# A written order for layer 0's first blocks, 17 pieces in layer 1, and idle products at the layers' borders

## The chip, the core and the metric

The kernel runs on one core of one Trainium2 chip. A core has five engines that work side by side, each through its own queue of instructions in order: TensorE (PE in the profile) multiplies matrices, VectorE (DVE) and ScalarE (ACT) work element by element, GpSimd (POOL) does the same more slowly, and SyncE (SP) starts transfers. A product needs its weights loaded first; such a load is an instruction of its own (PEld) and overlaps the products. Data lies in an on-chip memory of 128 partitions, products are written to a small accumulator memory (PSUM), and transfers to and from the large memory (DRAM) run on 16 DMA engines that all queues share. ScalarE, GpSimd and SyncE can each start transfers.

The metric is device time in microseconds (us) of one execution. Times are medians of several runs; the profile is one execution more.

## The reference, cut to what matters

The input x is 8 samples of 128 channels and 56 x 56 pixels, all float32. Four layers follow one another, each x = x + layer(groupnorm(x)):

```python
# layer 0: attention between windows of 8 x 8 pixels (49 windows a sample)
proj = xw @ W_qkv + b_qkv                                  # q, k, v of each pixel
logit = einsum('npc,nqc->npq', q_win * SCALE, k_win)       # window means
topk_logit, r_idx = top_k(logit, 4)                        # 4 windows for each window
attn = softmax(einsum('bmqc,bmkc->bmqk', q_h * SCALE, k_sel))   # 8 heads, 64 x 256
out = (attn @ v_sel + depthwise3x3(v) + lepe_b) @ W_o + b_o
# layer 1: batch norm, then a recurrence over the 3136 pixels of a sample
inp = tanhshrink(seq @ w_in.T + b_in);  xgate = inp @ w_ih.T + b_ih + b_hh
h = tanh(xg + h @ w_hh.T)                                  # 512 states, pixel after pixel
out = h @ w_out.T + b_out
# layer 2: masked 3 x 3 and 1 x 1 convolutions;  layer 3: a residual block of two 3 x 3 convolutions
```

The group norm takes groups of 4 channels: mean and variance of each sample and group.

## The kernel before

All of x stays on the chip in one tile, X, of 128 channels by 8 samples by 3136 pixels.

**The beginning of layer 0** (lines 65 to 152 and 549 to 569). SyncE's queue loads the eight samples of x, 1.6 MB each, sample by sample. ScalarE's queue loads the constants and weights. Sample 0 is then prepared in program order; which instruction each engine takes next is left to the scheduler of the framework. `measure` (line 186) gives statistics of seven strips of 448 pixels (`bn_stats`, line 194), the mean over a group by a product with the constant matrix gavg (line 200), the variance likewise (line 213), and one over the root by an integer estimate and three rounds of four GpSimd steps (lines 218 to 229). `preparation` (line 233) has, for each strip: `normal` writes the normalised strip in window order (xw, line 244) and its window sums (xm, line 249); `keys` multiplies and VectorE adds the bias (line 258); `image` gives v as an image, evicted by ScalarE and stored by GpSimd's queue (lines 271 and 277); `pixels` gives v by pixel rows, evicted by VectorE and stored by GpSimd's queue (lines 293 and 297). Then `means` and `route` give the window logits, the four best windows and their numbers as one row, selr (line 329). Three strips of queries (line 345) follow. All this goes through four PSUM banks in turn (`psum`, line 180).

**The loop of layer 0** (lines 672 to 730). It works on pairs of windows, 196 in all, with an order written out by hand for PE, ScalarE, VectorE and GpSimd. SyncE's queue is left to the scheduler. Turn p of the loop computes scores, maxima and exponentials of pair p + 1 (lines 461, 469, 474), transposes them (line 497), and multiplies values of pair p (line 516). `gather` copies the chosen keys with GpSimd (line 436) and loads the chosen value rows by SyncE's queue (line 438, 8 transfers a pair). `divisors` spreads reciprocal sums by GpSimd (rc, line 485), which PE then transposes (line 506). Around this, the work of preparing later samples, the depthwise products (line 375) and output projections (line 401) is placed by a planner: `job(ready, due, ...)` enters a piece of work with the first turn in which it can run and the last in which it must, and each turn has places for one product evicted by VectorE, one more, and a light one. `hook(p, f)` calls f in turn p. These pieces share one PSUM bank, "pp". The loop begins at FIRST = -2, two turns ahead of the first values.

**Layer 1** (lines 736 to 949). The recurrence is cut into NCH = 19 pieces of TC = 166 pixels, which run side by side: with 8 samples, a step has 19 x 8 = 152 columns. Each piece starts WARM = 56 pixels ahead, so there are 56 warming steps and 166 true ones, 222 in all. Inputs of a pixel (xn, pi, inp) are computed for two steps at a time (`prepare`, line 814). In the 56 warming steps the gate inputs are stored (gk, line 870), since the last 56 pixels of a piece are those that the next piece warmed up on, and they are read back for the last 56 steps (`recall`, line 841). A step with new inputs has 8 input products and 16 hidden-state products (line 858); a repeated one has 16 and adds the stored inputs with VectorE (v, line 884). Outputs (po, line 893) are two steps wide. Each float32 product is two records in the profile. Before the recurrence stands a chain of small steps for the two norms (lines 753 to 780).

**Layer 2** begins with the statistics of sample 0 (line 1010), the norm, and copies that spread each padded image over four row groups (`spread`, line 1046), by ScalarE, SyncE's queue and GpSimd's queue.

Of the kernel before, what the change touches and what calls it, by code (L numbers as in the profile page):

```python
# [18 lines left out]
P = 128  # L19
B = 8  # L20
# [14 lines left out]
NCH = 19  # L35
TC = 166
# [8 lines left out]
def conv_stack_kernel(ctx: ExitStack, tc: tile.TileContext, a: dict, out: bass.AP):  # L45
# [19 lines left out]
    for b in range(2):  # L65
        nc.sync.dma_start(X[:, b, :], a["x"][b])
    gavg = load_const("gavg", [P, P])
    for b in range(2, B):
        nc.sync.dma_start(X[:, b, :], a["x"][b])
    mv1 = const.tile([P, B, 2], F32, name="mv1")  # L70
    root = const.tile([P, 1], F32, name="root")
# [50 lines left out]
    with ExitStack() as l0:  # L122
# [8 lines left out]
        ident = load_const("ident", [P, P], c0)  # L131
        hmask = load_const("hmask", [P, 2], c0)
        own = load_const("own", [P, P], c0)
        wqkv = c0.tile([P, 3 * P], F32, name="wqkv")
        nc.scalar.dma_start(wqkv, a["L0_conv_W_qkv"])
        wo = c0.tile([P, P], F32, name="wo")
        nc.scalar.dma_start(wo, a["L0_conv_W_o"])
        bqkv = c0.tile([P, 3], F32, name="bqkv")
        nc.scalar.dma_start(bqkv, a["L0_conv_b_qkv"].rearrange("(c p) -> p c", p=P))
        bv_row = c0.tile([P, P], F32, name="bv_row")  # L140
        nc.scalar.dma_start(
            bv_row, a["L0_conv_b_qkv"][2 * P : 3 * P].rearrange("(o c) -> o c", o=1).broadcast_to((P, P))
        )

        wlep = c0.tile([3 * CL, 3, 4, CL], F32, name="wlep")
        nc.scalar.dma_start(wlep, a["lepe_d"])
        lb = c0.tile([P, 1], F32, name="lb")
        nc.scalar.dma_start(lb, a["L0_conv_lepe_b"].rearrange("(p o) -> p o", o=1))
        bo = c0.tile([P, 1], F32, name="bo")
        nc.scalar.dma_start(bo, a["L0_conv_b_o"].rearrange("(p o) -> p o", o=1))  # L150
        bqs = c0.tile([P, 1], F32, name="bqs")
        nc.vector.tensor_scalar(bqs, bqkv[:, 0:1], QSCALE, None, ALU.mult)
# [25 lines left out]
        bank = itertools.count()  # L178

        def psum(b, shape, name):  # L180

            if b == 0:
                return ps_s.tile(shape, F32, name=name, tag=f"s{next(bank) % 4}")
            return ps_p.tile(shape, F32, name=name, tag="pp")

        def measure(b):
# [11 lines left out]
            def mean_mm():  # L198
                st["pm"] = psum(b, [P, 1], f"pm0_{b}")
                nc.tensor.matmul(st["pm"], gavg, mv[:, 0:1], start=True, stop=True)  # L200
# [10 lines left out]
            def var_mm():  # L211
                st["pv"] = psum(b, [P, 1], f"pv0_{b}")
                nc.tensor.matmul(st["pv"], gavg, st["e"], start=True, stop=True)

# [16 lines left out]
            return stats, fill(mean_mm, mean_end), fill(var_mm, var_end)  # L231

        def preparation(b):
# [3 lines left out]
            xm = samp.tile([P, NWIN], F32, name=f"xm_{b}", tag="xm", bufs=1)  # L237
            kT = samp.tile([P, NWIN, WPX], F32, name=f"kT_{b}", tag="kT")
            ks[b] = kT

            def normal(i):

                wins = slice(i * NW, (i + 1) * NW)
                nc.vector.tensor_scalar(
                    xw[:, wins, :].rearrange("p j (u v) -> p j u v", v=WS),
                    X[:, b, i * BLK : (i + 1) * BLK].rearrange("p (u j v) -> p j u v", u=WS, v=WS),
                    st["gm"], st["r"], ALU.subtract, ALU.mult,
                )
                nc.vector.tensor_reduce(xm[:, wins], xw[:, wins, :], AX.X, ALU.add)

            def keys_mm(i):
                st["pk", i] = psum(b, [P, BLK], f"pk_{b}_{i}")
                nc.tensor.matmul(  # L253
                    st["pk", i], wqkv[:, P : 2 * P], xwf[:, i * BLK : (i + 1) * BLK], start=True, stop=True
                )

            def keys_end(i):
                nc.vector.tensor_scalar(
                    kT[:, i * NW : (i + 1) * NW, :].rearrange("p w x -> p (w x)"), st["pk", i],
                    bqkv[:, 1:2], None, ALU.add,  # L260
                )

            def image_mm(i):
                st["pv", i] = psum(b, [P, BLK], f"pvt_{b}_{i}")
# [4 lines left out]
            def image_end(i):  # L269
# [6 lines left out]
                later.append(  # L276
                    lambda: nc.gpsimd.dma_start(vimg[b % 2][:, 1 + i * WS : 1 + (i + 1) * WS, :], t)
                )

            def pixels_mm(n):  # L280

                st["vp", n] = psum(b, [P, 4, P], f"pvp_{b}_{n}")
# [6 lines left out]
            def pixels_end(n):  # L289
                w0, pv = 8 * n, st["vp", n]  # L290
                t = strip.tile([P, 4, P], F32, name=f"vp_{b}_{n}", tag="vp")
                if n < NW - 1:
# [4 lines left out]
                    later.append(lambda: nc.gpsimd.dma_start(dst, t))  # L297
                else:
                    nc.vector.tensor_tensor(t[:WPX, 0, :], pv[:WPX, 0, :], bv_row[:WPX, :], ALU.add)
                    later.append(lambda: nc.gpsimd.dma_start(vpix[b % 2][w0], t[:WPX, 0, :]))  # L300


            def means_mm():
                st["pw"] = psum(b, [P, 2, NWIN], f"pw_{b}")
# [10 lines left out]
            def route_mm():  # L315
                st["pl"] = psum(b, [NWIN, NWIN], f"pl_{b}")
                nc.tensor.matmul(st["pl"], st["qk"][0], st["qk"][1], start=True, stop=True)

            def route_end():
# [17 lines left out]
                fill(route_mm, route_end),  # L337
            )

        def queries(b, i):  # L340
            st = {}

            def mm():
                st["pq"] = psum(b + i, [P, BLK], f"pq_{b}_{i}")
# [76 lines left out]

        def gather(W):
# [4 lines left out]
            _, idx = nc.values_load_multi_w_load_instructions(  # L427
                selrs[b][0:1, w * TOPK : (w + 1) * TOPK],
# [1088 lines left out]
```

## Time and profile before

| what | us |
|---|---|
| median of 3 runs | 3679.45 (3677.51 to 3683.7) |
| the profiled execution | 3677.05 |
| its span, first to last instruction | 3675.1 |
| first scores of layer 0 start at | 64.10 |
| last products of layer 0's loop | 1395.45 to 1396.47 |
| first input product of layer 1 | 1406.40 |
| last output product of layer 1 ends | 2935.9 |
| first product of layer 2's convolution | 2950.86 |
| layer 3, to the end | from about 3154 |

The profile names an instruction by its line in the kernel, its engine, its operation, and the tiles out<-in. Times are counted from the span's start. In a row of the timeline the bracket at the end is the time for which the engine had been idle before it, and what released it. The granted clock of PE is 1.00 at full speed and 0.50 at half.

### The profile page before, as it was taken

To read this page: it belongs to the slowest core of one execution; us is meant where nothing else is said; L and a number is where in the kernel's file an instruction comes from. 1 tells how busy PE (TensorE), PEld (TensorE's weight loads), DVE (VectorE), ACT (ScalarE), POOL (GpSimd) and SP (SyncE) were. 2 spreads that over 40 slices of the span, in tenths; PEclk is the share of its full clock that TensorE was granted. 3 is DMA by queue.
4 is the path that set the end of the run, shared out by engine and by line. 5 is a ranking of instruction groups with operands and counts; after the bars stand their busy time and mean duration, and the time that the engine had idled before them with its cause. 6 is when DMAs were issued, how large, how long until landed. Compare 5 with 4: busy or idle time off the path is not lost.

```text
span 3675.1 us, 85966 instructions
## 1 busy us (share of the span) xinstructions
PE 3545.7 (96%) x30150; PEld 2914.9 (79%) x30150; DVE 1889.8 (51%) x3923; ACT 1654.2 (45%) x5149; POOL 1349.3 (37%) x3663
## 2 busy tenths in 40 slices
PE   5999999999999998999999999999999989999998
PEld 3666666666666667999999999999999833799998
DVE  5888888888878773222111111111122266757665
ACT  2787878888888883222222222222211154122222
POOL 3767667676766662111111111111000066323221
PEclk8999999999999999999999999999999999999999
DMA  5444444343434431111000000000022166100000
GB/s 208 108 107 108 110 104 107 100 117 101 118 102 114 122 93 57 49 45 49 21 1 1 1 1 1 1 1 1 18 59 59 45 168 169 34 23 23 31 21 34
DMA packets 195814, 241.74 MB, mean 66 GB/s; under 512 B 42480, under 2 KB 153520, under 8 KB 194352
## 3 DMA queue, kind: packets, MB, share of 16 engines
q1 hardware_dynamic: 160992, 125.99, 11.8%
q0 software_dynamic: 32576, 109.48, 11.3%
q8 instruction: 245, 4.01, 0.5%
q14 instruction: 193, 1.58, 0.2%
q10 hardware_dynamic: 1808, 0.68, 0.1%
HBM read 135.64 MB, written 69.39 MB: 56 GB/s over the span
## 4 chain that ended last, share of the span: by engine, by line
PE 84%; DVE 6%; ACT 4%; issue 3%; DMA 1%; POOL 1%; SPq 0%; DVEq 0%; ACTq 0%; POOLq 0%
PE ps L858 32%; PE pt L497 8%; PE pc3b L1221 7%; PE pc3a L1221 7%; PE s L461 5%; PE po L893 5%; PE po L516 4%; PE plep L375 3%; ACT e L474 3%; PE pc L1069 3%; PE pi L833 2%; DVE nmax L469 2%; PE pq L345 1%; PE pk L253 1%; PE pc L1077 1%
## 5 line engine op out<-in xcount | busy, mean ns | idle before, releaser
L858 PE MATMUL ps<-hs,w_gates 128*128 128x152 f32 x7040 | 948.0, 293 | 0.2 <-DVE gk L870 0.2
L858 PEld LDWEIGHTS ps<-hs,w_gates 128*128 128x128 f32 x7040 | 924.9, 190 | 8.3 <-issue 0.4
L474 ACT ACTIVATE e<-s,nmax 128x256 f32<-128x256 f32 x1568 | 732.3, 480 | 250.4 <-DVE nmax L469 246.7
L881 ACT ACTIVATE hs<-ps,bg 128x152 f32<-128x152 f32 x664 | 221.3, 384 | 932.2 <-PE ps L858 923.0
L836 DVE SCALAR_TENSOR_TENSOR inp<-pi,bine,th 128x304 f32<-128x304 f32 x166 | 83.0, 533 | 854.5 <-ACT th L835 854.5
L469 DVE TENSOR_REDUCE nmax<-s 128x2 f32<-128x512 f32 x784 | 501.0, 680 | 22.7 <-PE s L461 22.7
L497 PEld LDWEIGHTS pt<-c_ident,e 128*128 128x128 f32 x3136 | 353.1, 141 | 191.4 <-issue 103.0
L497 PE MATMUL pt<-c_ident,e 128*128 128x128 f32 x3136 | 450.6, 279 | 29.4 <-ACT e L474 10.2
L822 POOL TENSOR_TENSOR xn<-X,ctr 128x152 f32<-128x152 f32 (+1 forms) x164 | 92.1, 581 | 898.1 <-PE pi L833 893.6
L858 PEld LDWEIGHTS ps<-inp,w_gates 128*128 128x128 f32 x2656 | 363.4, 191 | 19.6 <-DVE inp L836 1.6
L858 PE MATMUL ps<-inp,w_gates 128*128 128x152 f32 x2656 | 372.8, 294 | 0.3 <-DVE inp L836 0.2
L474 ACT ACTIVATION_READ_ACCUMULATOR e<-s,nmax 128x1 f32 x1568 | 323.0, 206 | 0.0
L436 POOL COPY ks<-kT 128x64 f32 x1568 | 300.2, 237 | 17.8 <-PE s L461 12.0
L485 POOL TENSOR_TENSOR rc<-rden,c_own 128x128 f32<-128x128 f32 x392 | 148.4, 399 | 394.1 <-DVE rden L482 249.6
L499 DVE COPY eT<-pt 128x512 f32<-128x512 f32 x392 | 263.0, 671 | 19.6 <-PE pt L497 11.5
L1221 PE MATMUL pc3b<-vb,u_w2c_t 128*128 128x224 f32 x1344 | 257.6, 353 | 0.0
L1221 PE MATMUL pc3a<-va,u_w1c_t 128*128 128x224 f32 x1344 | 255.6, 353 | 1.4 <-DVE va L1211 1.4
L1221 PEld LDWEIGHTS pc3a<-va,u_w1c_t 128*128 128x128 f32 x1344 | 254.2, 190 | 1.5 <-POOL va L1210 1.5
L1221 PEld LDWEIGHTS pc3b<-vb,u_w2c_t 128*128 128x128 f32 x1344 | 253.6, 190 | 0.0
L461 PE MATMUL s<-ks,qm 32*128 32x256 f32 x3136 | 250.9, 403 | 0.1
L500 ACT COPY eT<-pt 128x512 f32<-128x512 f32 x392 | 235.8, 602 | 4.9 <-PE pt L497 3.6
L516 PE MATMUL po<-eT,vs 128*32 128x128 f32 x6272 | 226.4, 277 | 12.0 <-ACT eT L500 10.6
(224 smaller groups left out, 4400.2 us busy)
## 6 DMA issues: line engine op xcount, KB each, us to landing
vs<-vpix SPq DMA_DIRECT2D x1568, 32.0 KB, 2.1
kept<-gk SPq DMA_DIRECT2D x56, 304.0 KB, 2.1
g<-kept SPq DMA_DIRECT2D x56, 304.0 KB, 2.7
v<-vimg POOLq DMA_DIRECT2D x56, 290.0 KB, 4.0
v<-vimg POOLq DMA_DIRECT2D x56, 289.5 KB, 4.9
v<-vimg POOLq DMA_DIRECT2D x56, 289.0 KB, 5.8
vimg<-vrow POOLq DMA_DIRECT2D x56, 232.0 KB, 2.8
X<-in_x_dram SPq DMA_DIRECT2D x8, 1568.0 KB
```

Source lines behind the costliest of these rows:

```text
L436: nc.gpsimd.tensor_copy(kw[:, t : t + 1, :], ks[b][:, bass.ds(idx[t], 1), :])
L461: nc.tensor.matmul(s_["s"][g][:, o, :], w["qm"][h].rearrange("p h x -> p (h x)"), w["kw"][h], start=True, stop=True,)
L469: nc.vector.tensor_reduce(s_["nmax"][:, g, :], s_["s"][g], AX.X, ALU.max, negate=True)
L474: nc.scalar.activation(wins[2 * p + o]["e"][:, g, :], s_["s"][g][:, o, :], AF.Exp, bias=s_["nmax"][:, g, o : o + 1], accum_out=s_["den"][: ...
L497: nc.tensor.transpose(pt[c][:, g, :], s_["e"][:, g, c * P : (c + 1) * P], ident)
L499: nc.vector.tensor_copy(s_["eT"][0], pt[0])
L500: nc.scalar.copy(s_["eT"][1], pt[1])
L516: nc.tensor.matmul(po[ch, o, 0], s_["vw"][:, c, ch], s_["eT"][c][:, g, :], start=(c == 1), stop=(c == 0),)
L858: nc.tensor.matmul(ps[f][:, i], w, src, start=(i == 0 and k == 0 and h != fresh), stop=(k == KH - 1 if h else k == KI - 1 and (s < WARM or ...
L881: nc.scalar.activation(hs[f][:, s % 2, i], ps[f][:, i], AF.Tanh, bias=bg[:, m : m + 1])
L893: nc.tensor.matmul(po, wout[:, k, :], hs[k // 2][:, :, k % 2], start=(k == 0), stop=(k == KH - 1))
L1221: nc.tensor.matmul(m[k], u[:, dy, k, :], v[:, k, i * WS + dy : i * WS + dy + WS, :], start=(dy == 0), stop=(dy == 2),)
```

## The change

It has five parts.

1. Loads. Sample 0's x is loaded in four strips ahead of all else, sample 1's in two after the first constants. x of samples 2 to 7 is loaded strip by strip by GpSimd's queue (42 transfers), from hooks in the loop, eight turns ahead of its statistics. Some weights move from ScalarE's queue to SyncE's.
2. The beginning of layer 0 stands in an order written out for PE, ScalarE, VectorE and GpSimd, like the loop. Sample 0's root is ScalarE's Sqrt and a reciprocal. ScalarE normalises strips 1, 3 and 5 and evicts sample 0's keys. Means and route come right after the keys. Images 2 to 6, the last pixel strip and queries 1 and 2 come in the loop's first turns. Six PSUM banks are used in turn. Stores of this stage are SyncE's. The first four windows' value rows are loaded after the loop's second turn, by a `fetch` that is apart from `gather`.
3. NCH becomes 17 and TC 186: steps have 136 columns and are 242 in all, of which 186 have new inputs.
4. Idle products (`warm`), whose results are not read: at the start, before and after the group statistics of layer 1 (6 and 14) and of layer 2 (8 and 26). PE's order at the first border is written out, and `ctr` is computed earlier in the chain; the first inputs of layer 1 are GpSimd's instead of VectorE's.
5. Layer 2's statistics of sample 0 are taken during the recurrence, tile by tile as outputs are finished; two of eight remain after it.

```diff
-NCH = 19
-TC = 166
+NCH = 17
+TC = 186
...
+    for lo, hi in ((0, 2), (2, 4), (4, 6), (6, 7)):
+        load_x(0, lo, hi, nc.sync)
     gavg = load_const("gavg", [P, P])
-    for b in range(2, B):
-        nc.sync.dma_start(X[:, b, :], a["x"][b])
...
+        banks = itertools.cycle([(ps_s, f"s{k}") for k in range(4)] + [(ps_t, f"pt{k}") for k in range(2)])
+        begun = []
...
+            def first_root():
+                sd = small.tile([P, 1], F32, name="sd0", tag="sd1")
+                nc.scalar.activation(sd, st["pv"], AF.Sqrt, bias=eps)
+                st["r"] = small.tile([P, 1], F32, name="r0_0", tag="r0", bufs=4)
+                nc.vector.reciprocal(st["r"], sd)
+                st["off"] = small.tile([P, 1], F32, name="off", tag="off", bufs=1)
+                nc.vector.tensor_scalar(st["off"], st["gm"], st["r"], -1.0, ALU.mult, ALU.mult)
...
+        nc.scalar.activation(root, eps, AF.Sqrt)
+        warm(3, BLK)
+        warm(4, P)
+        stats, mean, var = made[measure, 0] = measure(0)
+        for i in range(NBLK):
+            stats(i)
+        run(mean)
+        warm(3, P)
+        run(var)
+        warm(5, P)
+        nc.vector.tensor_scalar(bqs, bqkv[:, 0:1], QSCALE, None, ALU.mult)
+        _, keys, image, pixels, means, route, normalise, sums = made[preparation, 0] = preparation(0)
+        for i in (1, 3, 5):
+            normalise(i, True)
+        for f, i in ((normalise, 0), (normalise, 2), (sums, 0), (sums, 1), (normalise, 4), (sums, 2), (sums, 3),
+                     (normalise, 6), (sums, 4), (sums, 5), (sums, 6)):
+            f(i)
+        for i in range(NBLK):
+            run(keys[i])
+        run(means)
+        pixels[0][0]()
+        run(route)
+        pixels[0][1]()
+        for f in (queries(0, 0), image[0], image[1], *pixels[1:-1]):
+            run(f)
+        nc.scalar.activation(root, eps, AF.Exp)
+        begun.append(True)
+        job(-1, -1, lambda: pixels[-1])
+        hook(-1, lambda: tails.extend(lambda f=f: run(f) for f in (queries(0, 1), image[2], image[3])))
+        for i in range(4, NBLK):
+            job(-1, min(pair_of(0, (i - 2) * NW) + 1, 2 * i), lambda i=i: image[i], True)
+        hook(-1, lambda: neighbours(0, 0))
...
+            at = [FIRST + (i > 2) for i in range(NBLK)] if b == 1 else [pair_of(b - 2, 0) + i for i in range(NBLK)]
+            if b > 1:
+                for i in range(NBLK):
+                    hook(max(at[i] - 8, FIRST + i // 2), lambda b=b, i=i: load_x(b, i, i + 1, nc.gpsimd))
...
+            if p == FIRST + 1:
+                for W in range(4):
+                    fetch(W)
...
+    def warm(n, psum, tag):
+        t = psum.tile([P, P], F32, name="warm", tag=tag)
+        for _ in range(n):
+            nc.tensor.matmul(t, gavg, gavg, start=True, stop=True)
...
+        borders.enter_context(tc.manual_schedule(engines={mybir.EngineType.PE}))
...
+        mean, var = mv1[:, :, 0], mv1[:, :, 1]
+        warm(6, ps_1, "pa")
         gm, d, pv = group_stats(mean, var, B, ps_1, "pa", "l1")
+        warm(14, ps_1, "pa")
         sd, r = inv_std(pv, B, "l1")
...
+                if done and s >= WARM and pixel(s) > done[0] + 1:
+                    stats(len(cuts) - 2 - len(done))
+                    if len(done) == 1:
+                        stats(len(cuts) - 2)
+                    done.pop(0)
...
+            for j in range(len(tiles) - 2, len(tiles)):
+                stats(j)
...
                 for i in range(NBLK):
                     norms[0].stats(i)
+                warm(8, ps_g, "pg")
                 norms[0].mean_mm()
                 norms[0].mean_end()
                 norms[0].var_mm()
+                warm(26, ps_g, "pg")
```

## The prediction

> **What bounds the kernel now.** I read the page first. TensorE (PE) is busy 96% of the span and 84% of the chain that ended last, so time falls only where PE waits, runs at half clock, or has fewer columns to stream. Then I read the busy time of stages. In the rows below the columns are the stretch, its length, busy time and instructions of PE, weight loads, VectorE, ScalarE and GpSimd, then the granted clock and the DMA.
>
> ```profile
> 0.00:1396.50 1396.50, 1308.04 (x15212) 881.53 (x15212) 1108.03 (x2176) 1090.49 (x3839) 910.54 (x2906) 0.99 0.43 114
> 1396.50:1417.70 21.20, 12.02 (x44) 9.60 (x45) 10.67 (x39) 5.22 (x12) 6.93 (x13) 0.60 0.07 27
> 1417.70:2935.90 1518.20, 1515.70 (x10684) 1443.20 (x10684) 277.47 (x658) 342.81 (x936) 166.12 (x343) 1.00 0.07 24
> 2935.90:2957.00 21.10, 6.74 (x35) 2.99 (x34) 13.85 (x31) 11.79 (x17) 14.70 (x29) 0.68 0.62 142
> ```
>
> Layer 1's recurrence (third row) is PE-bound to 99.8%. The borders before and after it (second, fourth) are chains of small steps at a low clock. Layer 0 needs its own look at the start. In time order, from the instruction timeline:
>
> ```profile
> 8.93 0.15 DVE L152 TENSOR_SCALAR bqs<-bqkv 128x1 f32<-128x1 f32 x1 [8.05 <-DMA bqkv<-in_L_conv_b_qkv_dram]
> 9.00 3.78 DVE L194 BATCH_NORM_STATS2 st<-X 128x6 f32<-128x448 f32 x7
> ...
> 22.68 1.39 DVE L244 TENSOR_SCALAR xw<-X,gm,r 128x448 f32<-128x448 f32 x2 [2.79 <-POOL r L229]
> ...
> 39.66 0.69 DVE L293 TENSOR_TENSOR vp<-pvp,bv_row 128x512 f32<-128x512 f32 x1 [5.34 <-DMA vpix<-vp]
> ...
> 58.46 0.91 SPq L329 DMA_DIRECT2D selr<-sel  x1
> ...
> 62.19 0.76 POOL L436 COPY ks<-kT 128x64 f32 x4 [1.55 <-DMA selr<-sel]
> ...
> 64.10 2.09 PE L461 MATMUL s<-ks,qm 32*128 32x256 f32 x16
> ```
>
> The first scores start at 64.10 us. Before them the statistics wait behind a 4-byte bias load, the normalisation for sample 1's statistics and twelve tiny GpSimd steps, and the value rows for a store that shares the DMA engines with all of x (some 420 GB/s until about 38 us in the DMA view). From 53.0 to 73.4 us the granted clock is 0.50.
>
> **Part A, the start.** Sample 0's x comes alone and in strips, so the seven statistics (3.78 / 7 = 0.54 us each) follow the strips. The DMA view moves its first 1.6 MB by 7 to 8.7 us, so I take the end of statistics as 8.1 and the aggregate (0.34) as 8.4. The group mean and variance cost what they cost now from 13.21 to 15.2 (2.0 us); then a Sqrt (0.27), a reciprocal (0.2) and the offset (0.2): normalisation begins at 11.0 instead of 22.68. ScalarE normalises three strips (0.69 each, as its 448-column eviction) and evicts the keys. VectorE has four normals of 0.73 and seven sums of 0.61: 7.2 us, to 18.3. Key products (0.92 at full clock) and seven ScalarE evictions (0.7) end near 18, hidden beside these sums. Means, first pixel product, route and maxima: the same instructions took 55.36 to 58.43 (3.1 us, of which the last products ran at half clock); 2.7 with the pixel product between, so the selection ends at 21.0. From its end to the first gathered key there are 3.76 us now (58.43 to 62.19), and 1.9 more to the scores: **26.7 us instead of 64.10, 37.4 gained**.
>
> Part of this comes back. What was left out of the beginning runs in pair 0's turn: last pixels, two queries, images 2 and 3, four statistics of sample 1. These share one PSUM buffer, so product and eviction alternate: VectorE has four maxima (2.7), four statistics (2.2) and the evictions (0.27 + 2 x 0.68); the second query is evicted 8.9 us after the scores began, then two images (2 x (0.95 + 0.7)) and the eight transposes (1.1): about 12.6 us to the next scores, where the trace has 7.13. So 5.5 go back. Images 4 to 6 add up to 0.7 of ScalarE in three later pairs, of which I let 0.9 in all show: **A = -31 us**. SyncE's own queue: the key selection must pass the stores of images and pixels, and 16 value fetches wait for the last pixel's store (31 us); at 0.65 us each plus 2.1 to landing the first eight are in by 39.4, the first value product is due near 42. If that slack of 2.5 were gone, it would be paid once. Bounds: -22 (the pairs after the start wait as long again as I count, 9 us) to -36 (nothing comes back but ScalarE's work).
>
> **Part B, 17 pieces.** Row widths go from 152 to 136 columns, steps with new inputs from 166 to 186, repeated ones stay 56.
>
> ```profile
> 2004.79 4.30 PE L858 MATMUL ps<-hs,w_gates 128*128 128x152 f32 x32
> 2008.92 1.19 PE L833 MATMUL pi<-xn,xw 128*128 128x304 f32 x4
> ...
> 31.79 1.05 PE L285 MATMUL pvp<-wqkv,xw 128*128 128x128 f32 x8
> ```
>
> A record at 152 columns starts (4.30 - 0.293) / 31 = 129.2 ns after the last, one of 304 every 255.8 ns: slope 0.833 ns a column, 2.5 ns fixed. So 115.8 ns at 136 and 229.2 ns at 272. Before: 7072 hidden-state records (7040 of the page and 32 of step 56, which reads another tile) + 2656 input records at 129.2, and 83 pairs x 12 at 255.8: 1256.6 + 254.8 = 1511.4 us. After: 241 x 32 + 186 x 16 = 10,688 at 115.8, 93 x 12 = 1116 at 229.2: 1238.0 + 255.8 = 1493.8. That is -17.6, if nothing but streaming counts. [...] The trace's own row decides: line 285 loads new 128-column weights for each record and its 128-column records are (1.05 - 0.29) / 7 = 109 ns apart, which is the same straight line. No surplus down to 128.
>
> Shorter products also hide less. In the first 56 steps the hidden-state products wait for two VectorE copies (gk, 0.66 us) after the first half of the input products. The cover of eight records shrinks by 0.107 us, the copies by 0.03: the wait of 0.05 us a step becomes 0.14, +5.0 us over 56. In the repeated steps PE waits for VectorE and ScalarE once in two steps:
>
> ```profile
> 2910.90 0.47 DVE L884 TENSOR_TENSOR v<-ps,g 128x304 f32<-128x304 f32 x1 [2.28 <-issue]
> 2911.41 0.46 ACT L885 ACTIVATE hs<-v 128x304 f32<-128x304 f32 x1 [3.65 <-DVE v L884]
> 2911.91 0.81 PEld L893 LDWEIGHTS po<-hs,xw 128*128 128x128 f32 x4 [0.31 <-ACT hs L885]
> ```
>
> The stall now is 0.345 a pair of steps; nine records shrink by 0.12, the chain by 0.07: 0.40, +1.5 over 28 pairs. **B = -11.1 us**, bounds -14 to 0 (waits three times as sensitive). The eight new statistics of layer 2's first sample lie in steps where VectorE is 82% idle; each would cost up to 0.55 if it fell ahead of v, 1 to 2 us at worst.
>
> **Part C, border 0 to 1.**
>
> ```profile
> 1397.90:1414.90 17.00, 9.36 (x27) 7.30 (x28) 7.61 (x32) 3.75 (x8) 4.47 (x9) 0.50 0.04 15
> ```
>
> Of these 17 us at half clock, products run from 1406.40 on. Until the first full step at 1417.72 there are 11.3 us; at full clock the same products and evictions need about 7.9: 3.4 to gain if idle products hold the clock. [...] Against it: beta's products now stand behind the last projection in PE's order, and six idle products (12 records of 109 ns, 1.3 us) stand ahead of the mean, which can be 0.4 to 1.8 late. In favour: two copies fewer ahead of the mean (0.37) and VectorE rid of the 0.85 us that the first inputs cost it, while GpSimd takes 1.0 instead of 0.86. **C = -3**, bounds -4.5 to 0.
>
> **Part D, border 1 to 2.** Seven statistics (3.78) become two (0.7): 3.1 earlier for normalisation. But the first block waits for SyncE, whose queue issues weights until 2945.43 before its first spread at 2945.52, and for its landing at 2950.8. GpSimd's thirty spreads do move by 3. **D = -2.5**, from 0 (SyncE's order keeps all) to -4 (clock kept too). The eight idle products end at about 2937.6, when the mean is not ready yet.
>
> **Part E, x of samples 2 to 7 on GpSimd.** 42 issues; the nearest row is a strip stored to DRAM by GpSimd, 0.59 us (line 407), 25 us in all. GpSimd waits 394 us ahead of its rc steps (line 485), and what is behind it in the queue, rc and the next gathers, has some 1.6 us before PE asks for it. I take a tenth: **E = +2**, bounds 0 and +25.
>
> **Sum:** -31 - 11.1 - 3 - 2.5 + 2 = -45.6. The profiled execution took 3677.05 us (span 3675.1), the runs' median is 3679.45; the same difference goes on the median: **3634 us**.
>
> **Rivals.** First, the beginning gains under half (22 or less comes off the pairs): sum -30 or -14 where nothing of it survives, 3650 to 3665. For it: first pairs are chains of waits, not PE. Against: nothing after 64 us depends on the absolute time, x included. Second, the pieces give nothing, since PE's waits grow as fast as the rows shrink: 3645. Against it: 55 of 83 fresh pairs show no wait at all. Third, the other side: GpSimd's strips stall the pair. If an issue waits for an earlier transfer to land and rc waits behind it, 42 strips x 2 us = 84 - 47.6 = +36: 3716. It decides at 47.6 / 42 = 1.13 us a strip (1.3 for 0.2% slower). For it: GpSimd is busy 65% of layer 0, with joins and image stores bunched in some pairs. Against: rc waits for another engine in nearly every pair (119 times for rden alone), and ahead of its gathers and neighbour loads GpSimd waits for DMA 4.3 us in all of layer 0. Fourth, better than I count: 3620.
>
> **How the numbers follow.** Forecast 0.62 (3620 to 3649), start below half 0.15, pieces nothing 0.12, strips stall 0.07, better still 0.04. 0.2% (7 us) is about what a measurement can tell from no change. Only the third rival and the far tail of the first end beyond it: faster 0.90, same 0.04, slower 0.06. Range 3615 to 3661.
>
> **What would show it.** First scores near 27 us and the second 12 us on; 136-column records 116 ns apart; waits of 0.14 ahead of hidden-state products in the first 56 steps; clock 1.00 over both borders; GpSimd's x issues near 0.6 us, with pair times unchanged at 6.7. First scores after 40, record spacing over 120 ns, or pairs over 7.5 us where strips are issued, would make it wrong.

## The result: 3634 us, and the profile after

| | before | after |
|---|---|---|
| median of 4 runs, us | 3678.48 (3676.59 to 3683.7) | 3634.15 (3627.78 to 3636.9) |
| profiled execution, us | 3677.05 | 3636.9 |
| its span, us | 3675.1 | 3635.1 |

The ratio is 0.9875, with a 95% interval from 0.9858 to 0.9892. The changed kernel is 44 us faster by the medians and 40.0 us by the two traces. Where the 40.0 us are, read from the starts of the same products in both traces:

| stretch | before | after | gained | forecast |
|---|---|---|---|---|
| span's start to first scores | 64.10 | 27.71 | 36.4 | 37.4 |
| first to second scores (pair 0's turn) | 7.13 | 16.76 | -9.6 | -5.5 |
| second scores to pair 13's | 82.93 | 85.35 | -2.4 | -0.9 |
| pair 13's scores to layer 0's last projection product | 1241.77 | 1241.62 | 0.15 | -2 |
| to the first hidden-state product of layer 1 | 21.79 | 17.05 | 4.7 | 3 |
| to the last output product (recurrence) | 1517.78 | 1506.69 | 11.1 | 11.1 |
| to layer 2's first block | 15.36 | 12.78 | 2.6 | 2.5 |
| layers 2 and 3 | 724.26 | 727.15 | -2.9 | 0 |

These are the stretches of the profile after, with the same columns as before: stretch, its length, busy time and instructions of PE, weight loads, VectorE, ScalarE, GpSimd, granted clock, DMA share, GB/s. The last two rows lie inside the first: pair 0's turn, and its part at half clock.

```profile
0.00:1372.00 1372.00, 1313.33 (x15254) 887.68 (x15254) 1102.90 (x2165) 1097.25 (x3853) 923.13 (x2927) 0.99 0.45 116
1372.00:1388.50 16.50, 11.96 (x73) 10.73 (x73) 9.62 (x35) 5.03 (x12) 7.24 (x15) 0.90 0.08 31
1388.50:2895.60 1507.10, 1503.65 (x11768) 1450.78 (x11769) 274.17 (x704) 355.26 (x1036) 172.98 (x391) 1.00 0.07 22
2895.60:2916.70 21.10, 16.89 (x124) 11.72 (x123) 11.98 (x31) 11.65 (x17) 17.71 (x36) 0.92 0.61 161
27.70:44.50 16.80, 11.29 (x39) 4.96 (x38) 9.32 (x18) 5.24 (x18) 6.44 (x19) 0.61 0.74 200
31.30:45.00 13.70, 9.62 (x20) 4.27 (x24) 5.78 (x12) 5.06 (x17) 4.60 (x12) 0.50 0.65 172
```

The recurrence is still bound by PE (1503.65 of 1507.10). The borders' clock rose from 0.60 and 0.68 to 0.90 and 0.92. The new low spot is pair 0's turn, at 0.61.

The beginning, from the timeline of the changed kernel (rows between are left out at `...`):

```profile
4.65 1.15 DVE L205 BATCH_NORM_STATS2 st<-X 128x6 f32<-128x448 f32 x2 [3.78 <-DMA X<-in_x_dram]
...
11.97 1.38 DVE L270 TENSOR_SCALAR xw<-X,gm,r 128x448 f32<-128x448 f32 x2
...
21.82 0.92 SPq L362 DMA_DIRECT2D selr<-sel  x1
...
24.88 0.76 POOL L474 COPY ks<-kT 128x64 f32 x4 [23.55 <-ACT vrow L302]
...
27.71 1.94 PE L504 MATMUL s<-ks,qm 32*128 32x256 f32 x16
```

The statistics now wait for strips of x, normalisation begins at 11.97 instead of 22.68 and the selection leaves at 21.82 instead of 58.46. The forecast had 11.0 and 21.0; the 1.0 us is there already at the end of the statistics (7.41 + 1.68 = 9.1 for 8.1). What follows in pair 0's turn, same timeline, is where a step of the forecast failed:

```profile
31.47 1.86 PE L380 MATMUL pq<-xw,wqkv 128*128 128x448 f32 x2 [1.46 <-DVE vp L332]
...
32.53 2.19 DVE L205 BATCH_NORM_STATS2 st<-X 128x6 f32<-128x448 f32 x4
...
35.02 0.61 DVE L384 TENSOR_SCALAR q<-pq,bqkv 128x448 f32<-128x448 f32 x1
...
35.69 1.86 PE L380 MATMUL pq<-xw,wqkv 128*128 128x448 f32 x2 [2.36 <-DVE q L384]
...
38.33 1.86 PE L296 MATMUL pvt<-xw,wqkv 128*128 128x448 f32 x2 [0.78 <-DVE q L384]
...
40.97 1.86 PE L296 MATMUL pvt<-xw,wqkv 128*128 128x448 f32 x2 [0.78 <-ACT vrow L302]
...
42.62 1.91 PE L540 MATMUL pt<-ident,e 128*128 128x128 f32 x8
```

Each product waits for the eviction of the one before, from the one buffer `pp`. PE is idle for 0.78 to 2.36 us ahead of them, the granted clock is 0.50 from 31.3 to 45.0 us, and each product takes 1.86 us where the forecast had 0.92 to 0.95, and the transposes 1.91 where it had 1.1.

The recurrence:

```profile
1975.31 3.87 PE L950 MATMUL ps<-hs,w_gates 128*128 128x136 f32 x32
```

The 32 records of 136 columns start (3.87 - 0.280) / 31 = 115.8 ns apart, as forecast (0.280 us is what the last record itself takes).

### The profile page after: what moved, and what is told of

It is laid out like the page before. It is cut to its first block, busy times and chain, and to the rows that moved or that the text cites. A ratio compares the mean times of both kernels' runs of the same rounds, so it can differ in the third digit from the quotient of the medians.

```text
span 3635.1 us, 88662 instructions
## 1 busy us (share of the span) xinstructions
PE 3548.4 (98%) x31368; PEld 2936.7 (81%) x31368; DVE 1878.2 (52%) x3949; ACT 1673.0 (46%) x5263; POOL 1368.3 (38%) x3734
## 4 chain that ended last, share of the span: by engine, by line
PE 86%; DVE 6%; ACT 5%; issue 3%; POOL 0%; DMA 0%; SPq 0%; POOLq 0%; DVEq 0%; ACTq 0%
PE ps L950 32%; PE pt L540 8%; PE pc3b L1327 7%; PE pc3a L1327 7%; PE s L504 5%; PE po L985 5%; PE po L559 4%; PE pc L1173 4%; PE plep L410 3%; ACT e L517 3%; PE pi L925 2%; DVE nmax L512 2%; PE pc L1181 1%; PE pq L380 1%; PE pk L283 1%
## 5 line engine op out<-in xcount | busy, mean ns | idle before, releaser
L950 PE MATMUL ps<-hs,w_gates 128*128 128x136 f32 x7680 | 932.9, 280 | 0.4 <-DVE gk L962 0.4
L950 PEld LDWEIGHTS ps<-hs,w_gates 128*128 128x128 f32 x7680 | 911.1, 190 | 8.6 <-issue 0.6
L973 ACT ACTIVATE hs<-ps,bg 128x136 f32<-128x136 f32 x744 | 237.3, 370 | 933.6 <-PE ps L950 926.1
L928 DVE SCALAR_TENSOR_TENSOR inp<-pi,bine,th 128x272 f32<-128x272 f32 x186 | 84.8, 497 | 888.7 <-ACT th L927 888.7
L540 PEld LDWEIGHTS pt<-ident,e 128*128 128x128 f32 x3136 | 354.3, 141 | 187.0 <-issue 104.3
L540 PE MATMUL pt<-ident,e 128*128 128x128 f32 x3136 | 449.6, 279 | 26.1 <-ACT e L517 7.5
L914 POOL TENSOR_TENSOR xn<-X,ctr 128x136 f32<-128x136 f32 (+1 forms) x186 | 96.3, 537 | 874.9 <-PE pi L925 871.1
L950 PE MATMUL ps<-inp,w_gates 128*128 128x136 f32 x2976 | 375.3, 279 | 0.7 <-DVE inp L928 0.7
L528 POOL TENSOR_TENSOR rc<-rden,own 128x128 f32<-128x128 f32 x392 | 147.7, 396 | 372.1 <-DVE rden L525 236.2
```

The source lines that it names most:

```text
L540: nc.tensor.transpose(pt[c][:, g, :], s_["e"][:, g, c * P : (c + 1) * P], ident)
L950: nc.tensor.matmul(ps[f][:, i], w, src, start=(i == 0 and k == 0 and h != fresh), stop=(k == KH - 1 if h else k == KI - 1 and (s < WARM or ...
L973: nc.scalar.activation(hs[f][:, s % 2, i], ps[f][:, i], AF.Tanh, bias=bg[:, m : m + 1])
```

## Experiments

The theory after the two traces: the start fell nearly 7 us short by one PSUM buffer and a clock of 0.50 in the turn in which PE waits for it; the pieces gave what streaming and two waits say; the borders gained by the idle products (first) and by the statistics (second); the strips of x cost nothing. Rivals stand with each run. Medians of the kernel before beside these runs were 3680 to 3681 us.

### The pieces alone

```diff
 # in the kernel before
-NCH = 19
-TC = 166
+NCH = 17
+TC = 186
```

> The kernel before with 17 pieces of 186 steps instead of 19 of 166 and nothing else. My theory (part B stands alone): the recurrence loses the same 11.1 us as in the trace of the changed kernel, 1518.2 to about 1507, so about 3667 us against 3678; records of 136 columns start 116 ns apart, and layers 0, 2 and 3 take what they took. Rival (the gain hangs on the rest, since the waits ahead of hidden-state products grow as the rows shrink): between 0 and -4 us. [...]

Measured: 3666.92 us, ratio 0.9965 (0.9951 to 0.9979). The recurrence runs from its first hidden-state product at 1418.24 to its last output product at 2925.04: 1506.8 us, against 1517.8 before and 1506.7 in the changed kernel. Part B stands alone and is worth 11.0 us. The median fell by 14; layers 2 and 3, which this kernel shares with the one before, took 720.6 us in its trace and 724.3 in that one's.

### Fewer pieces still: 16 and 15

```diff
-NCH = 17
-TC = 186
+NCH = 15        # the other run: 16
+TC = 210        #                198
...
-        CHUNK = 32
+        CHUNK = 36   #           34
```

> The changed kernel with 15 pieces of 210 steps (rows of 120 columns; statistics of layer 2 cut at 36 instead of 32). If the straight line of part B goes on (0.833 ns a column and 2.5 fixed): records 102.5 ns apart, 11840 of them and 105 x 12 of 202.5 make 1468.8 instead of 1493.8, 25 less; waits ahead of hidden-state products in the first 56 steps grow from 0.13 to 0.22 a step (+5), the repeated steps by 1.5: -18.5 us, about 3616. Rival: one weight load goes with each record, [...] below 128 columns of rows the load would set the spacing: [...] It decides whether 17 is near the fewest useful pieces.

> The changed kernel with 16 pieces of 198 steps (rows of 128 columns; statistics cut at 34). Theory after the run with 15: a weight load of 128 float columns keeps records 112 ns apart whatever the row: 11264 x 111.8 + 99 x 12 x 215.8 = 1515.7 us instead of 1493.8, +22, with a little more wait about +23. Rival (the surplus comes only below 128 columns, as the row of 128-column products of value pixels at 109 ns said in the forecast): 11264 x 109.2 + 256.4 = 1486.4, -7, with waits -4 us.

Measured: 3715.11 us (1.0099, 1.0082 to 1.0116) with 15, 3657.69 us (0.9942, 0.9926 to 0.9959) with 16; the recurrences took 1589.7 and 1528.9 us, 83 and 22.2 more than with 17. A row of the timeline of each, 15 pieces first:

```profile
2006.26 3.74 PE L950 MATMUL ps<-hs,w_gates 128*128 128x120 f32 x32
```

```profile
2007.34 3.74 PE L950 MATMUL ps<-hs,w_gates 128*128 128x128 f32 x32
```

Thirty-two records take 3.74 us at 120 columns and 3.74 at 128: (3.74 - 0.275) / 31 = 112 ns. The straight line of the forecast has 102.5 and 109.2. So neither row comes below 112 ns a record, the floor of these rows. The rival of the run with 15 named the weight load as what would set the spacing. With the 112 of these rows it gives 11840 x 111.8 + 105 x 202.5 x 12 / 1000 = 1323.7 + 255.2 = 1578.9 us, an estimate, against 1493.8: +85, where 83 were measured. What is the same in both runs is that each record brings a load of 128 columns of weights.

No run tried another weight size, but the changed kernel's trace has short rows that bear on it:

```profile
19.09 0.54 PE L339 MATMUL pw<-xm,wqkv 128*128 128x49 f32 x4
...
20.52 0.29 PE L350 MATMUL pl<-qkw,qkw 128*49 128x49 f32 x2
```

Both have rows of 49 columns, for which the straight line gives 43 ns. Where each record loads 128 columns of weights (`pw`, four records a sample), the third and the fourth record start 111 or 112 ns after the one before, in all 8 samples. Where it loads 49 (`pl`), the second starts 82 or 83 ns after the first, also in all 8. At an equal row of 49 columns the spacing is 82 or 83 ns with 49 columns of weights and 112 with 128, and with 128 it is 112 at rows of 120 and 128 too. That the load sets it is a reading of these rows, and not every load goes with it: the transposes (`pt`, line 540) load 128 columns too, but in a mean of 141 ns each where the recurrence's loads take 190, and most of their records stay on the straight line, 109 ns apart.

The narrower the rows, the more of the recurrence is filled with weight loads: they are busy 1443.2 of 1518.2 us with 19 pieces, 1450.8 of 1507.1 with 17 and

```profile
1386.50:2976.60 1590.10, 1587.34 (x13064) 1563.19 (x13065) 271.66 (x752) 375.29 (x1155) 180.70 (x427) 1.00 0.06 18
```

1563.2 of 1590.1 with 15. Of the four sizes run, 17 is the fastest, and its 116 ns lie only 4 above the 112 of the narrower rows; 18 was not run.

### A second PSUM bank in pair 0's turn

```diff
+        opening = itertools.cycle([(ps_p, "pp"), (ps_o, "po")])
...
-            pool, tag = (ps_p, "pp") if begun else next(banks)
+            pool, tag = next(banks) if not begun else next(opening) if len(begun) == 1 else (ps_p, "pp")
...
+            if p == 0:
+                begun.append(True)
```

> The changed kernel, but in pair 0's turn the tail products (two queries, images 2 and 3) alternate between two PSUM banks, one of which no other work uses yet. Theory (pair 0's turn is long because each product waits for the eviction of the one before, at a clock that the waits have let fall): the second scores come 12 to 13 us after the first instead of 16.8, and the whole becomes about 4 us shorter, 3630. Rival (VectorE's and ScalarE's own work sets that turn, four maxima, eight exponentials and four statistics): 16 us or more, no change of the time.

Measured: 3628.42 us (0.9859, 0.9843 to 0.9876). The second scores come 11.97 us after the first instead of 16.76. From the timeline (line numbers are one higher here):

```profile
31.41 1.02 PE L381 MATMUL pq<-xw,wqkv 128*128 128x448 f32 x2 [0.51 <-DVE vp L333]
...
34.96 1.21 DVE L385 TENSOR_SCALAR q<-pq,bqkv 128x448 f32<-128x448 f32 x2
...
35.62 3.19 PE L297 MATMUL pvt<-xw,wqkv 128*128 128x448 f32 x4 [3.19 <-DVE q L385]
...
39.62 1.15 PE L505 MATMUL s<-ks,qm 32*128 32x256 f32 x16
```

The second query no longer waits for the first one's eviction, and the two records of its product take 1.02 us, at a clock of 1.00. One wait of 3.2 us is left, for evictions that stand behind the four statistics in VectorE's order, and from its last 0.5 us on the clock is low here too, 0.50 from 35.1 to 38.5 us:

```profile
27.65:39.60 11.95, 8.11 (x35) 3.96 (x34) 8.85 (x18) 5.25 (x18) 6.47 (x19) 0.86 0.95 246
```

So VectorE's and ScalarE's own work did not hold the turn at 16 us, as the rival had it. Pair 13's scores start 95.85 us after the first ones, against 102.11: 6.3 gained, of which 4.8 in the turn and 1.5 in the pairs behind it.

### The clock alone: idle products in the turn

```diff
+            if p == -1:
+                idle(6)          # 128 columns each, in a bank of the transposes
             if two and not early:
                 two[0]()
...
-            for f in tails:
+            for f, n in zip(tails, (13, 3, 3)):
+                idle(n)
                 f()
```

> The changed kernel, but with idle products (6, 13, 3 and 3 of 128 columns, into a bank of the transposes) ahead of the tail products of pair 0's turn; the waits for the one bank are left as they are. Theory (what my sum missed is the clock of 0.50 between 31.3 and 45.0 us alone): the clock stays at 1.00, each of four tail products takes 0.93 instead of 1.86 and the transposes 1.1 instead of 1.9; second scores 12.5 to 13.5 us after the first, about 3630 in all. Rival (waits for the bank and VectorE's queue, not the clock): the second scores stay 16 us or more after the first although the clock is 1.00.

Measured: 3763.45 us (1.0225, 1.0208 to 1.0242), and this total says nothing of the question: the edit put idle products ahead of the tail products of every later turn of layer 0 that has such, so that 54 turns are 1.7 to 3.0 us longer, most of them 9.2 to 9.4 us instead of 6.4 to 6.6. Pair 0's turn can be read by itself:

```profile
32.54 3.06 PE L645 MATMUL idle<-c_gavg 128*128 128x128 f32 x26
...
35.22 0.62 DVE L384 TENSOR_SCALAR q<-pq,bqkv 128x448 f32<-128x448 f32 x1
...
35.89 1.02 PE L380 MATMUL pq<-xw,wqkv 128*128 128x448 f32 x2 [0.29 <-DVE q L384]
...
39.49 1.02 PE L296 MATMUL pvt<-xw,wqkv 128*128 128x448 f32 x2
...
40.34 1.04 PE L540 MATMUL pt<-ident,e 128*128 128x128 f32 x8
```

```profile
27.90:41.30 13.40, 12.75 (x85) 9.43 (x84) 8.95 (x18) 5.25 (x18) 6.49 (x19) 1.00 0.90 240
```

The waits for the one buffer are as long as they were (the first query is still evicted at 35.2), but the clock is 1.00 and each tail product takes 1.02. The second scores come 13.4 us after the first. So 3.4 of the 4.2 us that the forecast missed in this turn are the half clock. In this turn of the two traces the half clock goes with the pauses: in the changed kernel PE was busy 9.62 of the 13.7 us at 0.50, and with the pauses filled it is busy 12.75 of 13.4 at 1.00.

### Bank and idle products together

```diff
 # the second bank as above, and, in pair 0's turn only:
+            if p == -1:
+                idle(6)          # ahead of the first tail product, then 2 ahead of each
...
-                warm(26, ps_g, "pg")
+                warm(37, ps_g, "pg")
```

> The changed kernel with the second PSUM bank in pair 0's turn, a few idle products in that turn (6 ahead of the first tail product, 2 ahead of each next one, in this turn only) and 37 instead of 26 idle products ahead of layer 2's first block. If clock and bank are all that was missed in pair 0's turn: second scores about 11.5 us after the first, against 12.0 with the bank alone; first block of layer 2 at full clock, 1 us gained. In all 1 to 2 us under the kernel with the bank alone, 3626 to 3628. If the idle products come ahead of work that is due, or start too early to last: 0 to +1 us.

Measured: 3628.96 us (0.9862, 0.9846 to 0.9879), no less than with the bank alone (3628.42), so the 1 to 2 us were not there. The turn does what was expected:

```profile
28.98:39.98 11.00, 9.12 (x59) 6.30 (x58) 8.86 (x18) 5.24 (x18) 6.48 (x19) 1.00 0.98 254
```

Pair 0's turn in the four cases, in us, with the runs that follow below:

| | clock falls to 0.50 | idle products, clock 1.00 |
|---|---|---|
| one bank | 16.76 | 13.40 |
| two banks | 11.97 and 12.98 | 11.00 |

At full clock the second bank is worth 2.4 us (in a turn with fewer idle products), with one bank the clock 3.4. But the first scores started at 28.98 in this trace, and the first block of layer 2 came 13.8 us after the last output product instead of 12.9. The longer row of idle products brought nothing there.

### Borders without idle products

```diff
-        warm(6, ps_1, "pa")
         gm, d, pv = group_stats(mean, var, B, ps_1, "pa", "l1")
-        warm(14, ps_1, "pa")
...
-                warm(8, ps_g, "pg")
...
-                warm(26, ps_g, "pg")
```

> The changed kernel without the four sets of idle products at the borders of layers 1 and 2. Theory: they hold the clock; without them the products from the first input product to the first hidden-state product run at 0.50 again, 11 us instead of 7.3, so that stretch and its wait take 20 to 21 us after layer 0's last projection instead of 17.05, and the first block of layer 2 comes 1 to 1.5 us later after the last output product (12.8 now): +4 to +6 us in all. Rival (the borders gained by fewer copies and statistics and by GpSimd's share, and the idle products only take time ahead of what is due): -1 to +1 us.

Measured: 3636.34 us (0.9886, 0.987 to 0.9903), 2 us over the changed kernel's median, which is less than executions differ. The trace is clearer. From first input product to first hidden-state product, without and then with idle products:

```profile
1381.50:1391.10 9.60, 8.93 (x40) 7.26 (x41) 3.92 (x11) 3.01 (x8) 3.78 (x8) 0.69 0.07 29
```

```profile
1381.20:1388.50 7.30, 6.16 (x41) 5.25 (x41) 3.90 (x11) 2.98 (x8) 3.78 (x8) 1.00 0.10 38
```

After layer 0's last projection product the first hidden-state product comes at 20.28 instead of 17.05: the idle products are worth 3.2 of the 4.7 us of the first border. Without them the clock was 0.50 from 1370.4 to 1387.5. At the second border the clock is 1.00 with them until 2908.8, past the start of the first block at 2907.97, and without them it was 0.50 from 2903.0 to 2916.7; but there they are worth nothing: the first block comes after 12.74 us without and 12.78 with them, and layers 2 and 3 behind it took no longer (721.0 us). That part of the theory fell.

### Layer 2's statistics at the border again

```diff
-            norms = [Norm(0, "l2_0", known if held is not None else None), Norm(1, "l2_1")]
+            norms = [Norm(0, "l2_0"), Norm(1, "l2_1")]
```

> The changed kernel, but layer 2's first sample takes its statistics from seven instructions at the border again (the eight that are made during the recurrence stay, unused). Theory (part D is the statistics: seven, 3.8 us, instead of two, 0.7): first block of layer 2 15.4 us after the last output product starts, as in the kernel before, against 12.8; +2.6 us in all. Rival (SyncE's queue of weight loads holds the first block whatever the statistics do, and the 2.6 came from elsewhere): 12.8 to 13.3, no change.

Measured: 3635.04 us (0.9876, 0.986 to 0.9893). The first block comes 15.83 us after the last output product: 2.7 to 3.1 later than in the two traces of the changed kernel (12.78, 13.13). In its timeline

```profile
2896.71 3.77 DVE L1114 BATCH_NORM_STATS2 st_l<-X 128x6 f32<-128x448 f32 x7
...
2900.51 0.34 DVE L1116 BATCH_NORM_AGGREGATE mv_l<-st_l 128x2 f32<-128x42 f32 x1
...
2910.65 1.86 PE L1173 MATMUL pc<-g,w 96*32 96x448 f32 x5
```

the aggregate starts at 2900.51, 5.7 us after the last output record; in the changed kernel

```profile
2897.19 0.37 DVE L1116 BATCH_NORM_AGGREGATE mv_l<-st 128x2 f32<-128x48 f32 x1
...
2907.97 1.40 PE L1173 MATMUL pc<-g,w 96*32 96x448 f32 x6 [2.38 <-DMA g<-pad]
```

2.0 us after it (2897.19 for 2895.18). Part D is the statistics. The total hardly shows the 2.7 us: beside it on the same chip the changed kernel took 3631.0 (3629.8 to 3634.5), this one 3635.0 (3631.4 to 3637.0), and the ranges overlap.

### Strips of x in halves

```diff
-        cols = slice(lo * BLK, hi * BLK)
-        engine.dma_start(X[:, b, cols], a["x"][b][:, cols])
+        parts = 2 if b > 1 else 1
+        step = (hi - lo) * BLK // parts
+        for k in range(parts):
+            cols = slice(lo * BLK + k * step, lo * BLK + (k + 1) * step)
+            engine.dma_start(X[:, b, cols], a["x"][b][:, cols])
```

> The changed kernel with each of the 42 strips of x for samples 2 to 7 issued by GpSimd as two half strips: 84 issues, the same bytes. Theory after the trace (an issue costs GpSimd 0.6 us, in time in which it waits): 42 more issues change nothing, -1 to +1 us. What I had forecast (a tenth of an issue and more reaches TensorE): +2 to +4. The third rival of the forecast (an issue that holds up rc or the next gathers, 2 us each): +40 us or more, pairs of 8 us and over where strips go.

Measured: 3631.16 us (0.9869, 0.9852 to 0.9885). GpSimd's groups between 60 and 1350 us, changed kernel and then halves:

```profile
L68 POOL DMA_DIRECT2D X<-in_x_dram x35 | 20.0, 573 | 0.0
```

```profile
L71 POOL DMA_DIRECT2D X<-in_x_dram x70 | 38.7, 556 | 1.2 <-issue 1.2
```

Twice the issues of 0.56 us put 19 us more on GpSimd. From pair 13's scores to pair 195's it took 1229.36 us, against 1228.35 in the changed kernel and 1228.49 before; the other traces of the changed loop in which this stretch is as it was have 1228.1 to 1228.8. So of 19 us of added work about one shows on the path.

### The changed kernel and the second bank once more, on one chip

> The changed kernel as it is, beside the one with two banks on the same chip. If what layers 2 and 3 gave back in its trace (2.9 us) comes from how transfers fall in one execution and not from the change: 3632 to 3635 us as the median and layers 2 and 3 in 721 to 727 us; if the change costs it, 727 again.

> The kernel with two banks in pair 0's turn again, beside the changed one on the same chip. Theory: 5.9 us less to the last pair of layer 0, as in the first trace, and 5 to 6 us less in the median. Rival (the difference of the medians, 5.7, was one of chips and executions): under 3 us.

Measured: 3631.02 us (3629.77 to 3634.45) for the changed kernel, 3626.58 (3625.65 to 3628.26) with the second bank; ratios to before 0.9871 (0.9854 to 0.9887) and 0.9857 (0.9841 to 0.9874). From the first scores to pair 195's it is 1330.2 and 1324.9 us, 5.2 less (5.8 in the first pair of traces). The ranges don't meet, and the kernel with the bank beats the changed one by 4.4 us here and 5.7 in the first runs. It and the kernel that adds idle products to the bank are the fastest of all that ran.

In the same changed kernel layers 2 and 3 took 720.0 us here and 727.2 in the first trace:

```profile
2907.90:3635.10 727.20, 711.28 (x4206) 579.75 (x4206) 480.40 (x1020) 208.54 (x353) 253.89 (x380) 0.98 0.22 62
```

```profile
2909.10:3629.10 720.00, 705.27 (x4206) 580.10 (x4206) 480.02 (x1020) 208.45 (x352) 253.70 (x380) 0.99 0.22 62
```

PE's busy time differs by 6.0 us with the same 4206 instructions. So the 2.9 us that the changed kernel seemed to give back there lie within what two executions of one kernel differ by. In the first trace 23.2 us of this stretch were at half clock, in the later one 8.8, which goes with the difference; but it isn't all of it, since over all 13 traces the stretch takes 720.0 to 727.2 us, and the run with late statistics took 724.5 with 8.6 us at half clock.

## Why the prediction was right, and where its steps were not

The forecast was 3634 us and the median came out at 3634.15. That it hit within 1 us is luck. The traces' sum is -40.0 instead of -45.6: single terms were off and partly made up for each other. Besides, layers 2 and 3 alone make one execution differ from another by up to 7 us, and the changed kernel's median was 3631.0 when it ran again.

**A, the start: -31 forecast, -24.3 measured.** The first scores were 1.0 us late (27.71 for 26.7; 26.9 to 28.8 in six more traces with the same opening). The step that failed is "about 12.6 us to the next scores": 16.76. It had the order of products and evictions right, one buffer included. But it priced the products at the full clock, 0.95 us, and in this turn the clock was 0.50 from 31.3 us on. Three of the four products count. The first query's is hidden, since VectorE evicts it only behind the four statistics (at 35.0 us, and at 35.2 with the clock held); in the run with 16 pieces the half clock began only at 35.7, behind that product, and the turn was 16.76 as well. Three products at 1.86 instead of 0.95 and the transposes at 1.91 instead of 1.1 make 3.5 us, against 3.4 measured with the clock held. The other 0.8 (13.40 for 12.6) is not the clock: products of 1.02 us instead of 0.95 are 0.2 of it, an aggregate (0.34) that the sum leaves out ahead of the first eviction is some more, and the rest stays open. The pairs behind the turn lost another 2.4 instead of 0.9, with the clock at 0.50 again from 51.8 to 58.6; with the second bank, in whose traces the clock stays at 1.00 there, they lost 0.9 to 1.0. The third of A's risks, value fetches late on SyncE's queue, didn't show.

**B, the pieces: -11.1 forecast, -11.1 measured**, and -11.0 alone. The waits in the first 56 steps came to 7.8 us in the trace instead of 3.0, which is 0.14 a step as forecast. Most records of 136 columns are 115 or 116 ns apart, on the straight line (115.8). But the sentence "No surplus down to 128", that is, no spacing above that line, is wrong, and the row it rested on said so: the working took 0.29 us off for the last record, which is what a record of 152 columns takes. One of 128 takes 0.27:

```profile
33.44 0.27 PE L285 MATMUL pvp<-wqkv,xw 128*128 128x128 f32 x1
```

In that row of eight (31.79) the first gap is 109 ns and the other six are 111 or 112. At 136 columns the straight line still holds, 4 ns above the 112 of the narrower rows, and that the change stopped there is luck: by the straight line 16 pieces would have streamed for 7 us less than 17, and they cost 22 us more, which would have turned the sign of this part.

**C, the first border: -3 forecast, -4.7 measured**, just outside its bound of -4.5. The idle products gained 3.2, where the forecast had 3.4 for the clock, and 1.5 came without them (20.28 for 21.79). The cost set against it, a mean 0.4 to 1.8 us late behind beta's and idle products, did not come, since PE had both behind it before layer 0's last projection product. The clock wasn't 1.00 all over the border: it is 0.50 from 1376.2 to 1379.6, under the idle products themselves, with PE busy for all of these 3.40 us.

**D, the second border: -2.5 forecast, -2.6 measured.** The statistics explain it (2.7 to 3.1 when they are put back), and idle products neither helped nor hurt. SyncE's own first spread hardly moved, as the forecast had feared for the whole; before and after:

```profile
2945.52 5.45 SPq L1059 DMA_DIRECT2D g<-pad  x8
```

```profile
2904.69 4.42 SPq L1163 DMA_DIRECT2D g<-pad  x7
```

It starts 10.0 us after the last output product before and 9.5 after, right behind SyncE's loads in both. GpSimd's first spread moved from 9.2 to 6.1, and the first block now starts 3.3 us behind SyncE's spread instead of 5.3. Why the block follows that spread sooner was not tested.

**E, the strips: +2 forecast, 0 measured** (1228.35 against 1228.49 us over 182 pairs). A tenth of the issue time was too much; doubled issues show about a twentieth. The third rival is out: a pair takes 6.75 us in the mean before and after, and 14 pairs take over 7.5 us in both.

**The other rivals.** The start gained 24.3, so the first (22 or less) didn't come about, though not by much; the second is excluded by the run with the pieces alone; the fourth, 3620, was not reached; the kernel with the second bank comes nearest, 3627 to 3628.

## What to carry to other kernels

Where a chain is written so that each product waits for the eviction of the one before, don't price its products at the full clock without a row that shows it (here the clock was 0.50, and they took 1.86 us instead of 1.02), and look for a free bank first: here one spare bank in one turn was worth 4 to 6 us. Narrower rows paid along the straight line of streaming down to 136 columns here (115.8 ns), and no longer at 128 and 120 (112 ns both). So look in the trace for a row of the narrower width with the same weight load, and compute the width at which the line meets its spacing before choosing a size (about 131 columns here, an estimate from 0.833 ns a column, 2.5 fixed and 112). When a spacing is taken from a row's length, take off what its own last record takes. Effects of 2 to 3 us hardly show in a median of this kernel; read them from the start of the same product in two traces, and check that a stretch which the change doesn't touch is equally long in both.

## What the runs showed of the hardware

The stretches at half clock, in us from the span's start (in both traces there is one more, which the kernel's end cuts; the clock is on record from 29.2 us on before, from 7.4 after):

| before | after |
|---|---|
| 39.4 to 46.2 | 10.9 to 14.3 |
| 53.1 to 73.5 | 31.3 to 45.0 (pair 0's turn) |
| 1397.9 to 1415.0 (first border) | 51.8 to 58.6 |
| 2940.7 to 2954.4 (second border) | 1376.2 to 1379.6 (first border) |
| 3138.7 to 3145.5 | 2908.8 to 2912.2 (second border) |
| | 2963.4 to 2970.2 |
| | 3099.9 to 3106.7 |

They differ from one execution of a kernel to the next: in layers 2 and 3 of the changed kernel they come to 23.2 us in the first trace and to 8.8 in the later one. In pair 0's turn PE's longest pause between two products was 2.4 us. But the clock was 0.50 also where PE never paused: it was busy for all of the 6.80 us from 2963.4 to 2970.2. What starts a stretch and what sets its length was not shown.

That records of 120 and of 128 columns are spaced alike in the recurrence, at 112 ns, was not in the forecast, nor that the width in use after the change, 136, lies only 4 ns above this. Records of 49 columns with a load of 128 columns of weights (`pw`) come no sooner, at 111 or 112 ns.

One operation ran on GpSimd and on VectorE in the kernel before: `xn<-X,ctr` of 128x152 at the first border took 0.58 us on GpSimd and 0.41 on VectorE (medians).
